# A graph kernel's last edge groups, its code copies and its last norms: four groups instead of three at the end, copies on POOL, norms on DVE and ACT

## The chip, the cores and the metric

The kernel runs on one core of a Trainium2 chip. Times are microseconds of device time of one execution. Several runs of each kernel are made, and their median is what is compared; one more execution is taken with the hardware profiler, and all rows, timelines and waits below are of that one.

The engines are PE (matrix products), DVE and ACT (elementwise work), POOL (GpSimd: elementwise work, and it issues the indirect DMAs) and SP, whose queue issues nearly all other DMAs.

## The reference

There are N = 6250 nodes with 128 features, and E = 206250 edges with 128 features each. Every edge adds its features to its source node; the sum enters a small dense network, a residual and a layer norm.

```python
edge_aggr = jnp.zeros((n, HIDDEN), dtype=x.dtype).at[row].add(edge_features)
combined = jnp.concatenate([x, edge_aggr, global_expand], axis=-1) @ W_c + b_c
h = jax.nn.softplus(combined @ W1 + b1)
h = jax.nn.softplus(h @ W2 + b2)
y = h @ W3 + b3
out = _layernorm(x + y, axis=-1)
```

All data is float32. The edges come in no order of their source node.

## The kernel before

**Edges as columns.** The edges are laid out as 1612 columns of 128 (one edge in each partition; the last column holds 42). The nodes are cut into 25 blocks of 256. The first 48 columns are summed directly: for each, ACT builds a one-hot matrix over all nodes (`direct_hot`, L577 and L579) and PE multiplies (L589). The other 1564 columns go through groups.

**Groups.** `GROUPS` (L23) lists (columns, `sub`). For each group, DVE works out from the node numbers where each edge has to stand so that the edges are sorted by block, each block padded to whole chunks of `sub` x 128 rows (`node_codes` L205, `positions` L243, a list of small steps). POOL then scatters the rows of each column with an indirect DMA to a region of HBM, `place` (`scatter_rows` L638, the scatter itself on L644). There are three such regions, used in turn (`place_of`), so a group's scatters wait until the group three before it has been read. A column is scattered as 129 numbers: 128 features and the edge's code, which says which node of its block it belongs to, counted from a number of the group's own (`code_of` L188). The code is copied into the loaded row tile by `code_rows` (L632, ACT).

**Reduction.** When all scatters of a group have landed, its chunks are read back (`load` L400, up to eight columns of chunks in one DMA, five buffers), each code is compared with 256 numbers (`match` L409: DVE on L423 in one instruction for all columns; in the last two groups three of four loads on ACT, one instruction a column on L418 and one for all on L420; three buffers `hot`), PE multiplies (L437, two matrix instructions a column in float32) and DVE adds each chunk's product to its block in `sums_t` (L454; the block's place is read into registers, L448). Two chunks share one of three PSUM buffers (`SUMS`). With `sub` = 4 a load holds two chunks, with 2 four, with 1 eight, so the smaller `sub` is, the less padding there is and the more additions.

**The order.** The columns of a group are handled in pieces of ten (`LOAD_COLS`); 159 pieces in all. The loop on L698 goes through groups and pieces: for each piece it loads rows three pieces ahead, copies codes two pieces ahead and scatters the piece; between pieces it spreads, each list by its share of the group's pieces (`AHEAD`): the next group's positions (`prep`), the reduction of the group before (`sums`), the direct work in groups 1 to 6, and other steps. PE, DVE, ACT and SP execute in the order written here; POOL's order is left to the framework. All DMAs of SP have one order. After the loop the last group is reduced (L738).

**Dense layers.** 13 tiles of 512 nodes (one of 106) go through two softplus layers and a last product (`z_of`, `decay`, `log1p`, `softplus`, `last_layer`), on PE, ACT and DVE. The tiles are in parts of 4, 3, 3, 2 and 1. When a part's last tile is through, `norm` (L814) works out the inverse deviations on DVE by a chain of twelve small instructions, then scales all blocks of the part: on POOL (L833), for the last part on DVE. Each tile then goes out by one or two DMAs.

Of the kernel before, what the change touches and what calls it, by code (L numbers as in the profile page):

```python
# [7 lines left out]
F32 = mybir.dt.float32  # L8
BF16 = mybir.dt.bfloat16
I32 = mybir.dt.int32  # L10
U8 = mybir.dt.uint8
AF = mybir.ActivationFunctionType
# [4 lines left out]
P = 128  # L17

BL = 2 * P
LOAD_COLS = 10  # L20
EPS = 1e-5

GROUPS = ((40, 1), (120, 2), (200, 4), (240, 4), (240, 4), (240, 4), (212, 4), (140, 2), (88, 2),  # L23
          (44, 1))
CHUNK_ROWS = 1024
# [22 lines left out]
def kernel(  # L48
# [36 lines left out]
    for size, sub in GROUPS:  # L85
        c1 = min(TC, c0 + size)
        if c1 > c0:
# [12 lines left out]

    iota_f = const.tile([P, WIDE], F32, name="iota_f")
    nc.gpsimd.iota(iota_f, pattern=[[1, WIDE]], base=0, channel_multiplier=0,
                   allow_small_or_imprecise_dtypes=True)
# [64 lines left out]
    with ExitStack() as phase:  # L168
# [74 lines left out]
        def positions(g):  # L243
# [5 lines left out]
            in_block, so_far, got = {}, {}, {}  # L249
            pos = per.tile([P, C_MAX], I32, name="pos")  # L250
            pos_of[g] = pos
# [102 lines left out]
            def chunk_map():  # L354

                small = ps.tile([P, 4, P], F32, name="small", bufs=2)
                end_t = per.tile([NB, 1], F32, name="end_t")
                nc.tensor.transpose(small[:NB, 0, :], got["end"], ident)
                nc.vector.tensor_copy(end_t, small[:NB, 0, :1])
                ended = per.tile([NB, NSC_MAX], F32, name="ended")  # L360
                nc.vector.tensor_scalar(ended[:, :nsc], chunk_i[:, :nsc], end_t, None,
                                        op0=ALU.is_ge)
                offs = per.tile([1, NSC_MAX], I32, name="offs", bufs=3)
                offs_of[g] = offs
                flat = ps.tile([P, 4, P], F32, name="small", bufs=2).rearrange("p a b -> p (a b)")
                nc.tensor.matmul(flat[:1, :nsc], ones[:NB, :1], ended[:, :nsc],
                                 start=True, stop=True)
                nc.vector.tensor_scalar(offs[:, :nsc], flat[:1, :nsc], float(NB - 1), float(BL),
                                        op0=ALU.min, op1=ALU.mult)
# [22 lines left out]
        def reduce_steps(g):  # L392
# [16 lines left out]
            def match(i):  # L409
# [3 lines left out]
                hot_of[i] = hot  # L413
                if g > G - 3 and i % 4 != 3:

                    codes = iota_f[:, int(code_of(g)):int(code_of(g)) + BL]
                    for j in range(m):
                        nc.scalar.activation(hot[:, j], codes, AF.Abs,  # L418
                                             bias=chunks[i][:, j, D:W], scale=-1.0)
                    nc.scalar.activation(hot[:, :m], hot[:, :m], AF.Relu, bias=ones[:, :1],  # L420
                                         scale=-1.0)
                    return
# [122 lines left out]
        def direct_steps():  # L545
# [26 lines left out]
            def compare(c, w, q):  # L572
                n = min(WIDE, NB * BL - w * WIDE)
                hot = direct_p.tile([P, QUAD, WIDE], F32, name="direct_hot", bufs=4)
                hot_of[c, w, q] = hot
# [56 lines left out]
        def code_rows(i):  # L632
            if i >= len(pieces):
                return
            g, c, k, r = pieces[i]
            nc.scalar.copy(rows_at[i][:r, :k, D:W], low[:r, c:c + k].unsqueeze(2))  # L636

# [14 lines left out]
        with tc.manual_schedule(engines={ET.PE, ET.DVE, ET.Activation, ET.SP}):  # L652
# [22 lines left out]
            node_codes(ND, c1)  # L675
            for i in range(LEAD - 1):
                code_rows(i)
            for step in positions(0):
# [11 lines left out]
            left = [0.0] * G  # L690
            for g in range(1, G - 3):
                left[g] = max(0.0, groups[g][1] - groups[g][0]
                              - groups[g - 1][3] * groups[g - 1][2] / 3 - (9 if 3 <= g < 6 else 0))
# [4 lines left out]
            for g in range(G):  # L698
                mine = [q for q in range(len(pieces)) if pieces[q][0] == g]
                prep = []  # L700
                if g + 1 < G:
                    prep = [lambda g=g: node_codes(*groups[g + 1][:2])] + positions(g + 1)
                sums = reduce_steps(g - 1) if g else []
# [8 lines left out]
                for q in mine:  # L712
                    load_rows(i + LEAD)
                    code_rows(i + LEAD - 1)
                    scatter_rows(i)
# [30 lines left out]
    order = tiles[-1:] + tiles[:-1]  # L746
    parts = [order[:4]] + [order[i:i + 3] for i in range(4, len(order) - 3, 3)]
    parts += [order[len(parts) * 3 + 1:-1], order[-1:]]
    h1, h2, sub_z, x_of = {}, {}, {}, {}
# [64 lines left out]
    def norm(now, last):  # L814
# [9 lines left out]
        for _ in range(3):  # L824
            nc.vector.tensor_mul(t, g, g)
            nc.vector.scalar_tensor_tensor(t, t, -0.5, v, op0=ALU.mult, op1=ALU.mult)
            nc.vector.scalar_tensor_tensor(g, t, 1.5, g, op0=ALU.add, op1=ALU.mult)  # L827

        engine = nc.vector if last else nc.gpsimd
        for n0, w, y, at in now["done"]:  # L830
            for lo, hi, r in blocks(w):
                for q in range(lo, hi):
                    engine.tensor_scalar(y[:r, q, :], y[:r, q, :], mv[:r, at + q, 0:1],  # L833
                                         rs[:r, 1, at + q:at + q + 1],
                                         op0=ALU.subtract, op1=ALU.mult)
                m0 = n0 + lo * P
# [60 lines left out]
```

## Time and profile before

| what | value |
|---|---|
| median of 3 runs | 2163.95 us (2160.82 to 2169.29) |
| the profiled execution's own time | 2166.67 us |
| its span | 2164.9 us |
| mean granted TensorE clock | 0.925 |
| PE, PE weight loads | 1789.7 us (83%), 1209.0 us (56%) |
| DVE | 1328.0 us (61%) |
| ACT | 912.7 us (42%) |
| POOL | 1560.2 us (72%) |
| scatters | 1564, the first at 25.57, the last at 2018.42 |
| first layer's first product | 2086.08 |

How to read the rows: a group of instructions is given as line, engine, operation, tile written and tiles read, then the number of instructions, a bar, their busy time in us and the mean duration of one in ns, a second bar, and the idle time of the engine just before them with what ended most of it. "issue" is time in which the engine waited for nothing that the profile shows. A row of a timeline is start, duration, engine, line, operation, tiles, shapes, the number of instructions that it merges, and in brackets the idle time before with what ended it. The row of digits gives the busy share in tenths in 40 equal slices of the span, some 54 us each. Matrix products are pipelined and their ends are modelled.

### The profile page before, as it was taken

Reading aid. Unit: us, or ns where it says so; the run is one execution under the profiler, and the core shown is the slowest. Engines: PE = TensorE matmul, PEld = TensorE weight load, DVE = VectorE, ACT = ScalarE, POOL = GpSimd, SP = SyncE. Lnnn points to the kernel's source line nnn. Section 1 sums busy time; section 2 is a strip of 40 time slices with the busy share of each in tenths; the row PEclk is TensorE's granted clock in tenths of the full one; section 3 lists DMA queues with packets and bytes.
Section 4 is the critical chain, followed back from the end, with each engine's and each line's share of the span. In section 5 each row is a group of like instructions: output and inputs, shape, how many; then the busy total and the mean of one; then the engine's idle time right before and its main releaser. Section 6 shows DMA issues by size and latency. Waiting matters only on the chain.

```text
span 2164.9 us, 22230 instructions
## 1 busy us (share of the span) xinstructions
PE 1789.7 (83%) x6415; PEld 1209.0 (56%) x6415; DVE 1328.0 (61%) x1923; ACT 912.7 (42%) x1350; POOL 1560.2 (72%) x1631
## 2 busy tenths in 40 slices
PE   3398788966889878999889998788998899688884
PEld 0144445534555555666556666556666778566752
DVE  7386457524656345675465855355755798796567
ACT  0476665653444335444353443353342000006964
POOL 5777777777777767777777777777777777777226
PEclk8699999987999999999999999999999999899997
DMA  9998788738786665676756666556766687776521
GB/s 299 303 313 270 216 256 251 231 101 262 213 225 189 194 193 148 188 207 188 198 173 180 194 190 175 169 167 189 202 198 170 211 245 227 214 213 199 151 75 60
DMA packets 415376, 435.50 MB, mean 201 GB/s; under 512 B 37743, under 2 KB 305766, under 8 KB 415254
## 3 DMA queue, kind: packets, MB, share of 16 engines
q1 hardware_dynamic: 365062, 330.71, 54.9%
q0 software_dynamic: 50048, 103.35, 14.4%
q8 instruction: 51, 0.84, 0.2%
q14 instruction: 71, 0.58, 0.1%
q10 hardware_dynamic: 144, 0.02, 0.0%
HBM read 260.90 MB, written 173.03 MB: 200 GB/s over the span
## 4 chain that ended last, share of the span: by engine, by line
PE 57%; DVE 15%; POOL 9%; issue 7%; DMA 6%; ACT 4%; DVEq 1%; SPq 0%; POOLq 0%; ACTq 0%
PE part L437 37%; PE direct_sum L589 16%; POOL place L644 8%; DVE hot L423 7%; DMA place<-rows,pos 4%; DVE sums_t L454 2%; ACT hot L418 2%; DVE so_far L316 1%; DVE sums_t L593 1%; DMA rows<-in_edge_attr 1%; DMA chunks<-place 1%; PE small L339 1%; POOL y L833 1%; DVEq L448 1%; DVE pos L350 1%
## 5 line engine op out<-in xcount | busy, mean ns | idle before, releaser
L644 POOL DMA_INDIRECT place<-rows,pos x1564 | 1503.2, 961 | 509.0 <-issue 443.5
L437 PE MATMUL part<-hot,chunks 128*128 128x256 f32 x4472 | 1106.0, 405 | 267.8 <-DVE hot L423 250.9
L437 PEld LDWEIGHTS part<-hot,chunks 128*128 128x128 f32 x4472 | 894.9, 203 | 507.8 <-DVE hot L423 310.5
L577 ACT ACTIVATE direct_hot<-iota_f,less 128x512 f32<-128x512 f32 (+1 forms) x624 | 404.6, 695 | 811.0 <-PE direct_sum L589 808.1
L423 DVE SCALAR_TENSOR_TENSOR hot<-chunks,iota_ps 128x2048 f32<-128x2048 f32 (+1 forms) x261 | 592.2, 2270 | 44.2 <-DMA chunks<-place 44.2
L589 PE MATMUL direct_sum<-direct_hot,direct_rows 128*128 128x512 f32 (+1 forms) x1248 | 559.0, 580 | 29.4 <-DMA direct_rows<-in_edge_attr 25.6
L454 DVE TENSOR_TENSOR sums_t<-sums_t,part 128x256 f32 x781 | 327.1, 419 | 133.3 <-PE part L437 110.8
L589 PEld LDWEIGHTS direct_sum<-direct_hot,direct_rows 128*128 128x128 f32 x1248 | 233.3, 190 | 232.2 <-issue 204.9
L579 ACT ACTIVATE direct_hot<-direct_hot,ones 128x1024 f32<-128x1024 f32 (+1 forms) x312 | 348.0, 1115 | 10.1
L593 DVE TENSOR_TENSOR sums_t<-sums_t,direct_sum 128x512 f32<-128x512 f32 (+1 forms) x52 | 34.7, 667 | 410.5 <-PE direct_sum L589 410.5
L636 ACT COPY rows<-src_i 128x10 f32<-128x10 f32 (+1 forms) x159 | 30.7, 196 | 360.3 <-DMA place<-rows,pos 328.9
L350 DVE TENSOR_REDUCE pos<-at 128x20 int32<-128x500 f32 (+2 forms) x80 | 87.0, 1087 | 2.7
L316 DVE TENSOR_TENSOR_SCAN so_far<-iota_ps,ib 128x1500 bf16<-128x1500 f32 (+5 forms) x29 | 85.7, 2955 | 0.0
L418 ACT ACTIVATE hot<-iota_f,chunks 128x256 f32<-128x256 f32 x156 | 64.2, 493 | 26.7 <-DMA chunks<-place 24.2
L845 POOL TENSOR_TENSOR x_sb<-x_sb,b_all 128x512 f32<-128x512 f32 (+1 forms) x13 | 15.2, 1219 | 67.8 <-DMA x_sb<-in_x 67.8
L348 DVE TENSOR_TENSOR at<-small,ib 128x500 f32<-128x500 f32 (+2 forms) x80 | 52.9, 661 | 4.2 <-PE small L339 3.5
L833 POOL TENSOR_SCALAR y<-y,mv,rs 128x128 f32<-128x128 f32 (+1 forms) x45 | 35.2, 796 | 19.9 <-DVE rs L827 19.0
L262 DVE TENSOR_TENSOR ib<-block,iota_ps 128x1500 bf16<-128x1500 bf16 (+5 forms) x29 | 44.2, 1550 | 0.0
L273 PE MATMUL small<-ib,ones_h 128*128 128x500 bf16 (+2 forms) x80 | 23.8, 406 | 23.9 <-DVE ib L262 23.9
L536 DVE TENSOR_SCALAR z_x<-small,z_bias 128x512 f32<-128x512 f32 (+1 forms) x13 | 9.3, 718 | 51.3 <-PE small L534 51.3
L335 PE MATMUL small<-so_far,ones_h 128*128 128x500 bf16 (+2 forms) x80 | 31.4, 393 | 11.1 <-DVE last L319 11.1
L420 ACT ACTIVATE hot<-hot,ones 128x2048 f32<-128x2048 f32 (+1 forms) x20 | 39.2, 1960 | 0.7
(115 smaller groups left out, 472.7 us busy)
## 6 DMA issues: line engine op xcount, KB each, us to landing
chunks<-place SPq DMA_DIRECT2D x278, 516.0 KB, 4.5
rows<-in_edge_attr SPq DMA_DIRECT2D x155, 640.0 KB, 6.7
place<-fill SPq DMA_DIRECT2D x252, 258.0 KB, 8.3
place<-rows,pos POOLq DMA_INDIRECT x1564, 4.5
x_sb<-in_x SPq DMA_DIRECT2D x24, 256.0 KB, 4.6
direct_rows<-in_edge_attr SPq DMA_DIRECT2D x4, 768.0 KB
out<-y SPq DMA_DIRECT2D x12, 256.0 KB, 2.2
chunks<-place SPq DMA_DIRECT2D x3, 258.0 KB, 3.2
```

What stands on the lines that cost most here:

```text
L316: nc.vector.tensor_tensor_scan(t, iota_ps[:, 1:2].to_broadcast([P, NB * n]), in_block[k][0], 0.0, op0=ALU.mult, op1=ALU.add)
L350: nc.vector.tensor_reduce(pos[:, a - c0 + j0:a - c0 + j1], at.rearrange("p b g -> p g b"), axis=mybir.AxisListType.X, op=ALU.add)
L418: nc.scalar.activation(hot[:, j], codes, AF.Abs, bias=chunks[i][:, j, D:W], scale=-1.0)
L423: nc.vector.scalar_tensor_tensor(hot[:, :m], chunks[i][:, :m, D:W].to_broadcast([P, m, BL]), code_of(g), iota_ps.unsqueeze(1).to_broadcast ...
L437: nc.tensor.matmul(part[:, s - q, :], t[:, s * sub + j, :D], hot[:, s * sub + j], start=(j == 0), stop=(j == sub - 1))
L454: nc.vector.tensor_add(here, here, part[:, s - q, :])
L577: nc.scalar.activation(hot[:, j, :n], iota_f[:, :n], AF.Abs, bias=less[:, w, c + q + j:c + q + j + 1], scale=-1.0)
L579: nc.scalar.activation(hot[:, :, :n], hot[:, :, :n], AF.Relu, bias=ones[:, :1], scale=-1.0)
L589: nc.tensor.matmul(sum_of[c, w][:, :n], rows_in[c][:, q + j, :], hot[:, j, :n], start=(q + j == 0), stop=(q + j == k - 1))
L593: nc.vector.tensor_add(here, here, sum_of.pop((c, w))[:, :n])
L644: s = nc.gpsimd.indirect_dma_start(out=dst, out_offset=bass.IndirectOffsetOnAxis(ap=at, axis=0), in_=rows[:r, j, :], in_offset=None)
L833: engine.tensor_scalar(y[:r, q, :], y[:r, q, :], mv[:r, at + q, 0:1], rs[:r, 1, at + q:at + q + 1], op0=ALU.subtract, op1=ALU.mult)
```

## The change

- The groups after the sixth are (226, 4), (130, 2), (72, 2), (38, 1), (18, 1) instead of (212, 4), (140, 2), (88, 2), (44, 1). There are eleven groups instead of ten.
- The positions of group 8 are worked out in the stage of group 6 already, and those of groups 9 and 10 two stages ahead (`SOONER`). A third position buffer and a fourth offset buffer hold them.
- ACT matches in the last three groups: every other load in the first of them, three of four in the last two (`TAIL`). The row of numbers that codes are compared with gets 768 entries instead of 512, and `direct_hot` three buffers instead of four to make room.
- Codes are copied by POOL instead of ACT, for each piece just before its scatters in the program.
- The dense part's parts are 4, 3, 3 and 3 tiles. In the last one the blocks are scaled by DVE and ACT in turn; ACT needs the negative mean times the inverse deviation (`minus`), one more small instruction.

```diff
-GROUPS = ((40, 1), (120, 2), (200, 4), (240, 4), (240, 4), (240, 4), (212, 4), (140, 2), (88, 2),
-          (44, 1))
+GROUPS = ((40, 1), (120, 2), (200, 4), (240, 4), (240, 4), (240, 4), (226, 4), (130, 2), (72, 2),
+          (38, 1), (18, 1))
+SOONER = 6
+TAIL = (2, 4, 4)
...
-    iota_f = const.tile([P, WIDE], F32, name="iota_f")
+    iota_f = const.tile([P, len(TAIL) * BL], F32, name="iota_f")
...
-            pos = per.tile([P, C_MAX], I32, name="pos")
+            pos = per.tile([P, C_MAX], I32, name="pos", bufs=3)
...
-                if g > G - 3 and i % 4 != 3:
+                share = TAIL[g - G] if g >= G - len(TAIL) else 1
+                if i % share != share - 1:
...
-                hot = direct_p.tile([P, QUAD, WIDE], F32, name="direct_hot", bufs=4)
+                hot = direct_p.tile([P, QUAD, WIDE], F32, name="direct_hot", bufs=3)
...
         def code_rows(i):
-            if i >= len(pieces):
-                return
             g, c, k, r = pieces[i]
-            nc.scalar.copy(rows_at[i][:r, :k, D:W], low[:r, c:c + k].unsqueeze(2))
+            nc.gpsimd.tensor_copy(rows_at[i][:r, :k, D:W], low[:r, c:c + k].unsqueeze(2))
...
-            for i in range(LEAD - 1):
-                code_rows(i)
...
-                if g + 1 < G:
-                    prep = [lambda g=g: node_codes(*groups[g + 1][:2])] + positions(g + 1)
+                for k in range(g + 1 + (g > SOONER), min(G, g + 2 + (g >= SOONER))):
+                    prep += [lambda k=k: node_codes(*groups[k][:2])] + positions(k)
...
                     load_rows(i + LEAD)
-                    code_rows(i + LEAD - 1)
+                    code_rows(i)
                     scatter_rows(i)
...
-    parts = [order[:4]] + [order[i:i + 3] for i in range(4, len(order) - 3, 3)]
-    parts += [order[len(parts) * 3 + 1:-1], order[-1:]]
+    parts = [order[:4]] + [order[i:i + 3] for i in range(4, len(order), 3)]
...
-        engine = nc.vector if last else nc.gpsimd
+        if last:
+            minus = work.tile([P, 16], F32, name="minus")[:, :nb]
+            nc.vector.scalar_tensor_tensor(minus, mv[:, :nb, 0], -1.0, g,
+                                           op0=ALU.mult, op1=ALU.mult)
...
-                    engine.tensor_scalar(y[:r, q, :], y[:r, q, :], mv[:r, at + q, 0:1],
-                                         rs[:r, 1, at + q:at + q + 1],
-                                         op0=ALU.subtract, op1=ALU.mult)
+                    k = at + q
+                    if last and q % 2:
+                        nc.scalar.activation(y[:r, q, :], y[:r, q, :], AF.Identity,
+                                             bias=minus[:r, k:k + 1], scale=g[:r, k:k + 1])
+                        continue
+                    (nc.vector if last else nc.gpsimd).tensor_scalar(
+                        y[:r, q, :], y[:r, q, :], mv[:r, k, 0:1], g[:r, k:k + 1],
+                        op0=ALU.subtract, op1=ALU.mult)
```

The range over which direct work is spread keeps the groups 1 to 6 (`G - 4` for `G - 3`).

More of the change, by code (lines that the diff above doesn't have):

```diff
@@ L98 @@
     dram = ctx.enter_context(tc.tile_pool(name="dram", bufs=1, space=bass.MemoryType.DRAM))
-    iota_f = const.tile([P, WIDE], F32, name="iota_f")
-    nc.gpsimd.iota(iota_f, pattern=[[1, WIDE]], base=0, channel_multiplier=0,
+    iota_f = const.tile([P, len(TAIL) * BL], F32, name="iota_f")
+    nc.gpsimd.iota(iota_f, pattern=[[1, len(TAIL) * BL]], base=0, channel_multiplier=0,
                    allow_small_or_imprecise_dtypes=True)
@@ L362, in chunk_map @@
                                         op0=ALU.is_ge)
-                offs = per.tile([1, NSC_MAX], I32, name="offs", bufs=3)
+                offs = per.tile([1, NSC_MAX], I32, name="offs", bufs=4)
                 offs_of[g] = offs
@@ L690 @@
             left = [0.0] * G
-            for g in range(1, G - 3):
+            for g in range(1, G - 4):
                 left[g] = max(0.0, groups[g][1] - groups[g][0]
```

## The prediction

> **What bounds the kernel now.** I read the page first, for the share of each engine and its row in forty slices.
>
> ```profile
> span 2164.9 us, 22230 instructions
> ...
> POOL 5777777777777767777777777777777777777226
> ...
> L644 POOL DMA_INDIRECT place<-rows,pos x1564 | 1503.2, 961 | 509.0 <-issue 443.5
> ...
> L454 DVE TENSOR_TENSOR sums_t<-sums_t,part 128x256 f32 x781 | 327.1, 419 | 133.3 <-PE part L437 110.8
> ...
> L636 ACT COPY rows<-src_i 128x10 f32<-128x10 f32 (+1 forms) x159 | 30.7, 196 | 360.3 <-DMA place<-rows,pos 328.9
> ```
>
> PE is busiest (83%), but POOL's row does not move: seven tenths in every slice until the 37th, then almost nothing. The timeline of POOL tells why.
>
> ```profile
> 25.57 1.20 POOL L644 DMA_INDIRECT place<-rows,pos  x1 [18.45 <-DMA w_sb<-in_L_gnn_W]
> 27.08 0.96 POOL L644 DMA_INDIRECT place<-rows,pos  x1 [0.31 <-issue]
> ...
> 801.28 0.96 POOL L644 DMA_INDIRECT place<-rows,pos  x1 [0.30 <-issue]
> 811.52 0.96 POOL L644 DMA_INDIRECT place<-rows,pos  x1 [9.28 <-ACT rows L636]
> 812.78 0.96 POOL L644 DMA_INDIRECT place<-rows,pos  x1 [0.30 <-issue]
> ...
> 2017.16 0.96 POOL L644 DMA_INDIRECT place<-rows,pos  x1 [0.31 <-issue]
> 2018.42 0.91 POOL L644 DMA_INDIRECT place<-rows,pos  x1 [0.30 <-issue]
> 2086.94 0.45 POOL L845 TENSOR_TENSOR x_sb<-x_sb,b_all 106x128 f32<-106x128 f32 x1 [67.61 <-DMA x_sb<-in_x]
> ```
>
> One scatter starts every 1.265 us (2017.16 to 2018.42), busy 0.96 and 0.30 in which it waits for nothing shown. 1564 of them run from 25.6 to 2019.3. The sum of real waits in that stretch is about 15 us: 9.28 here, 1.46 at 1432.7 (both for the code copy on ACT), 4.63 at 81.2 (a load of rows). So POOL alone sets when the last edge is placed, although the chain of waits gives it 9%; PE, DVE and ACT have slack until then. The span is 25.6 of start, 1993.8 of scatters, 66.6 until the last sum is added (2085.9), and 79.0 of the dense layers.
>
> For the 66.6 us I read the timelines of ACT and DVE.
>
> ```profile
> 1969.43 3.30 ACT L418 ACTIVATE hot<-iota_f,chunks 128x256 f32<-128x256 f32 x8 [24.15 <-DMA chunks<-place]
> 1972.76 2.00 ACT L420 ACTIVATE hot<-hot,ones 128x2048 f32<-128x2048 f32 x1
> ```
>
> ```profile
> 1957.08 2.28 DVE L423 SCALAR_TENSOR_TENSOR hot<-chunks,iota_ps 128x2048 f32<-128x2048 f32 x1
> 1959.27 1.85 DVE L454 TENSOR_TENSOR sums_t<-sums_t,part 128x256 f32 x4
> 1961.04 2.28 DVE L423 SCALAR_TENSOR_TENSOR hot<-chunks,iota_ps 128x2048 f32<-128x2048 f32 x1
> ...
> 2065.20 3.88 DVE L454 TENSOR_TENSOR sums_t<-sums_t,part 128x256 f32 x8 [0.45 <-PE part L437]
> 2069.53 3.81 DVE L454 TENSOR_TENSOR sums_t<-sums_t,part 128x256 f32 x8 [0.45 <-PE part L437]
> 2073.80 1.85 DVE L454 TENSOR_TENSOR sums_t<-sums_t,part 128x256 f32 x4 [0.45 <-PE part L437]
> ...
> 2084.08 1.86 DVE L454 TENSOR_TENSOR sums_t<-sums_t,part 128x256 f32 x4 [0.20 <-DVE sums_t L454]
> ```
>
> Per load of eight columns: a match on ACT takes 5.23 us, on DVE 2.19 start to start; PE needs 3.57 (64 multiplications in 14.27). In groups of two columns a chunk DVE turns a load round in 3.96 when it matches too; in single chunks its eight adds take 4.3 and the match comes on top. ACT runs without a gap from 1969.4 to 2069.1 and then DVE's adds are last.
>
> **The code copies.** This decides the sign. They leave ACT (159, 0.196 us each, and 329 us in which ACT stood before them) and join the one queue that has no slack. What ACT gains is worth only what POOL waited for it: 9.28 + 1.46 less two usual gaps of 0.30 = **10.1 us** off. The 4.63 us for rows stays. What the copies add on POOL, no row shows. The nearest by size is the IOTA of 128x13 (142 ns, writes only); from the tensor additions (454 ns at 128 elements, 1.22 us start to start at 512: 2.0 ns an element) ten elements would come to 0.22. The scatter behind a copy has to wait for it, and a scatter that ACT released at 811.25 (its copy's end) began at 811.52: 0.27 after. That replaces the 0.30 it would have had anyway. So a copy that starts as the scatter ends costs 0.14 + 0.27 - 0.30 = 0.11; with 0.22 busy, 0.19. The bounds: 0, if it runs inside the 0.30 of the scatter before (below nothing is excluded: no work leaves POOL); and 0.30 + 0.22 + 0.27 - 0.30 = 0.49, if it too starts only after such a gap. Compute instructions that follow one another on POOL leave none (the normalisations start every 0.785 us at 0.796 busy), so I take the row nearest in size: 0.11 x 159 = **17.5 us**, between 0 and 78.
>
> The Trainium skill speaks against the lower bound. "Perfetto Trace Analysis", section "GPSIMD Engine Instruction", says that spans of this engine are not to be trusted and that start-to-start spacing is. By the rows there are 0.30 us idle per scatter to hide a copy in, and the edit is free; by the rule the 1.265 is all work and each copy is paid. I go with the rule, hence 0.11 rather than 0. "SBUF — State Buffer", section "Who interferes with whom", adds that a GpSimd instruction that reads SBUF is blocked by a DVE one with two SBUF inputs. Copies read, scatters' times hardly vary. Here such DVE work is rare (L199, L202, L298: 0.2 to 0.3 us, three a group); matches and adds read one operand from PSUM. By the rule at worst thirty collisions of 0.3 us, 9 us; by that share of DVE's time under 1. I add nothing.
>
> A copy waits for its load of rows, with all later scatters queued behind it, but those waited for the same load before. At the start the copies' inputs are there by 9.2, scatters begin at 25.6: nothing.
>
> **The groups.** Padding makes 2262 columns of products, 26 more: 12 us of PE over the run, hidden in stages that POOL paces. Only the end counts (numbers from zero; the 0.11 is in POOL's times).
> - Group 7 (130) has 89 chunks, 23 loads. Before, 24 loads and the positions of 44 columns took DVE 111.1 us (1858.6 to 1969.7), from 6.3 after the last scatter. Now one load and three quarters of another go, 7 us, and the positions of 18 columns cost some 3 less: 101. POOL needs 72 x 1.265 + 0.9 = 92 for group 8. So group 7's sums end 15 after that group's last scatter (6 before the change).
> - Group 8 (72): 60 chunks, 15 loads, half matched on ACT (5.23 per two) and half on DVE: PE's 3.57 bounds, 54 us. It ends 69 later; POOL's groups 9 and 10 take 48.5 + 23.1 = 71.6. So 3 us before the last scatter.
> - Groups 9 and 10 (38, 18): 62 + 42 single chunks. DVE: 12 full loads of 4.27, rests of 3.3 and 1.4, three matches of 2.19: 62.6. ACT: 11 matches, under 57, earlier begun; PE: 104 x 0.446 = 46. DVE is last.
> The sums end 60 us after the last scatter instead of 66.6: **6.5 off**. Fewer single columns are left over than the shift suggests: 104 single chunks take the place of 68.
>
> Group 6 grows by two loads and its positions' stage takes in group 8's; its backlog of some 20 us of PE at the start of the next stage (direct sums until 1691) could push all this by 5; bounds of the 6.5 are 0 and 15.
>
> **Buffers.** A position buffer more and one `direct_hot` less: nothing. A compare takes ACT 2.45 us, and 314 steps in some 1590 us leave 5 between two; ACT stands 808 us before that buffer as it is. Without that cover PE would fall behind and scatters would wait for the place of three groups ago. The wider iota is 0.27 us at 0.8, first read at 9.1: nothing. Earlier positions move DVE work inside POOL's time.
>
> **Norms.** The chain before the last tile (2148.3 to 2150.9) goes, so its addition starts 2.6 earlier; then 12 reciprocal roots (2.4 as at 2138.4), one more small operation (0.2), twelve blocks, six each on DVE (0.33 a start) and ACT (about 0.3, from 0.28 for 106 columns): 2.0. Normalisation ends at about 2154.8, not 2157.5 (POOL's last); one output issue instead of two is left behind it (0.92 for two). **3 off**; 0 to 4, since three tiles now leave at once.
>
> **The sum.** +17.5 - 10.1 - 6.5 - 3 = -2.1. The profiled execution took 2166.67, 1.8 outside its span; it would be 2164.6. The median of the runs is 2.7 lower: 2163.95 - 2.1 = **2162**.
>
> **The rivals.** *The copy breaks the queue (slower).* Each copy starts only after a scatter's full gap, or reads slower than the small rows: 0.30 us each is 47.7, so +28 and 2192; at the bound of 0.49 it is 2222. It decides from 0.124 us a copy (19.6 / 159), and from 0.19 it is visible. For it: scatters leave 0.30 after themselves without exception. Against: sequencer waits run while a scatter runs, and small POOL instructions follow closely. *Copies vanish in the gap (faster).* At zero, -19.6 and 2144. If DVE's adds also keep up with PE (46 for 62.6), the tail loses 16 more: 2128. For it: 0.30 idle as shown; against: the rule above, and 4.3 a load measured. *The split doesn't help:* if the backlog of groups 6 to 8 eats the 6.5, 2168; no sign change.
>
> **Chances.** A measurement tells 0.5% (10.8 us) from no change. Likeliest, copies of 0.05 to 0.18: 2152 to 2174, chance 0.37. Queue broken, above that: 0.32. Copies nearly free, or a shorter tail: 0.31. The range takes in most of both others, 2142 to 2193.
>
> **What would show it.** The spacing between the last scatter of a piece and the first of the next, less 1.265, times 159, is the copies' price. Waits for ACT rows must be gone and the last scatter end near 2027. After it the sums should take 60, with DVE's adds last; the stretch from there to the end 76. I am wrong if a copy costs over 0.19 or the sums take under 50.

## The result, and the profile after

Over 12 runs each the changed kernel took 2157.81 us (2154.09 to 2160.67) and the kernel before 2163.51 (2158.13 to 2169.29): a ratio of 0.9973, interval 0.9962 to 0.9984, or 5.7 us less. The forecast was 2162, with 2.1 us off. The profiled execution took 2160.67 with a span of 2158.9, at a granted clock of 0.941 (0.925 before).

| stretch, profiled, us | before | forecast | after |
|---|---|---|---|
| end of the last scatter | 2019.3 | 2026.7 | 2020.0 |
| from there to the last sum | 66.6 | 60 | 68.1 |
| from the last sum to the end of the span | 79.0 | 76 | 70.7 |

So the total was near, and all three rows are off in these two profiles, by 6.7, 8.1 and 5.3 us, the middle one against the other two: the last scatter came earlier than forecast, the stretch after it did not shrink, and the end took less. How far the granted clock bears on such times is not settled: of 26 executions of the kernel before on one chip the six at a clock under 0.935 took no longer than the others (medians of 2169.0 and 2168.5 us), of 21 on another the eight under it took 4 us longer (2172.1 and 2167.9).

The views that answer to those of before: first POOL's waits (wait, total us, times, longest), one row of the kernel before and then the changed kernel.

```profile
POOL place L644 <- ACT rows L636: 12.3, 7, 9.3
```

```profile
POOL place L647 <- issue: 412.5, 1353, 0.3
...
POOL place L647 <- POOL rows L639: 19.0, 122, 0.2
...
POOL place L647 <- DMA rows<-in_edge_attr: 5.6, 1, 5.6
```

No row for ACT is left; in its place stand 122 short waits of a scatter for POOL's own copy. POOL's timeline shows one:

```profile
1996.26 0.96 POOL L647 DMA_INDIRECT place<-rows,pos  x1 [0.30 <-issue]
1997.23 0.20 POOL L639 COPY rows<-src_i 128x7 f32<-128x7 f32 x1
1997.59 0.98 POOL L647 DMA_INDIRECT place<-rows,pos  x1 [0.16 <-POOL rows L639]
1998.87 0.96 POOL L647 DMA_INDIRECT place<-rows,pos  x1 [0.30 <-issue]
...
2019.14 0.90 POOL L647 DMA_INDIRECT place<-rows,pos  x1 [0.31 <-issue]
```

The copy starts when the scatter ends, takes 0.20 to 0.21, and the next scatter follows 0.16 later. That 0.37 stands where 0.30 of gap would have been: the spacing is 1.33 (1996.26 to 1997.59) and not 1.263. Over 112 single copies the median price is 0.063 us; the framework placed 16 pairs (0.183 each) and a few larger bunches. All copies together cost some 11 us.

Then DVE at the end of the sums: group 6's last addition and group 7's first match, first in the kernel before, then in the changed kernel, where the last additions follow.

```profile
1850.31 0.42 DVE L454 TENSOR_TENSOR sums_t<-sums_t,part 128x256 f32 x1 [0.85 <-PE part L437]
...
1858.64 2.29 DVE L423 SCALAR_TENSOR_TENSOR hot<-chunks,iota_ps 128x2048 f32<-128x2048 f32 x1 [4.00 <-DMA chunks<-place]
```

```profile
1865.64 0.42 DVE L459 TENSOR_TENSOR sums_t<-sums_t,part 128x256 f32 x1 [0.85 <-PE part L442]
...
1868.34 4.48 DVE L428 SCALAR_TENSOR_TENSOR hot<-chunks,iota_ps 128x2048 f32<-128x2048 f32 x2
...
1971.00 2.28 DVE L428 SCALAR_TENSOR_TENSOR hot<-chunks,iota_ps 128x2048 f32<-128x2048 f32 x1
...
2083.11 3.81 DVE L459 TENSOR_TENSOR sums_t<-sums_t,part 128x256 f32 x8 [0.46 <-DVE sums_t L459]
2087.31 0.88 DVE L459 TENSOR_TENSOR sums_t<-sums_t,part 128x256 f32 x2 [0.39 <-DVE sums_t L459]
```

In the changed kernel group 6's last addition is at 1865.6, group 7 begins at 1868.3 and fills DVE for 102.7 us until 1971.0, and the last addition ends at 2088.2. In between PE works through group 8 without a pause (240 products), and group 9's first load follows:

```profile
1971.04 52.07 PE L442 MATMUL part<-hot,chunks 128*128 128x256 f32 x240 [0.61 <-ACT hot L425]
2023.40 3.72 PE L442 MATMUL part<-hot,chunks 128*128 128x256 f32 x16 [0.29 <-ACT hot L425]
```

These are nearly the lengths that the prediction gave (101, 54 and 62.6 us; measured 102.7, 52.1 and 63.6, from 2024.6 on). Above all the start of the chain was later than assumed. Group 7's last scatter ended at 1852.4 before and at 1857.2 after the change. Before, group 6's sums were through by then (1850.7) and group 7 began 6.2 us later; after, they ended 8.8 us past it and group 7 began 11.1 us later.

### The profile page after: what moved, and what is told of

Its sections match the earlier page's. It is cut to its first block, busy times and chain, and to the rows that moved or that the text cites. A ratio compares the mean times of both kernels' runs of the same rounds, so it can differ in the third digit from the quotient of the medians.

```text
span 2158.9 us, 21792 instructions
## 1 busy us (share of the span) xinstructions
PE 1804.2 (84%) x6470; PEld 1217.8 (56%) x6470; DVE 1351.9 (63%) x1976; ACT 889.6 (41%) x1186; POOL 1583.0 (73%) x1782
## 4 chain that ended last, share of the span: by engine, by line
PE 57%; DVE 15%; POOL 9%; DMA 8%; issue 6%; ACT 3%; SPq 1%; DVEq 1%; ACTq 0%; POOLq 0%
PE part L442 39%; PE direct_sum L594 14%; POOL place L647 8%; DVE hot L428 7%; DMA place<-rows,pos 4%; DVE sums_t L459 3%; DMA place<-fill 3%; DVE sums_t L598 1%; SPq L149 1%; DMA rows<-in_edge_attr 1%; ACT hot L423 1%; DVE so_far L320 1%; PE small L343 1%; DVEq L453 1%; ACT away L776 0%
## 5 line engine op out<-in xcount | busy, mean ns | idle before, releaser
L442 PE MATMUL part<-hot,chunks 128*128 128x256 f32 x4524 | 1117.4, 405 | 245.7 <-DVE hot L428 237.3
L442 PEld LDWEIGHTS part<-hot,chunks 128*128 128x128 f32 x4524 | 905.4, 203 | 484.7 <-DVE hot L428 294.3
L428 DVE SCALAR_TENSOR_TENSOR hot<-chunks,iota_ps 128x2048 f32<-128x2048 f32 (+1 forms) x266 | 602.6, 2266 | 45.5 <-DMA chunks<-place 45.5
L594 PE MATMUL direct_sum<-direct_hot,direct_rows 128*128 128x512 f32 (+1 forms) x1248 | 562.9, 582 | 35.2 <-DMA direct_rows<-in_edge_attr 26.3
L459 DVE TENSOR_TENSOR sums_t<-sums_t,part 128x256 f32 x808 | 338.0, 418 | 99.9 <-PE part L442 74.2
L594 PEld LDWEIGHTS direct_sum<-direct_hot,direct_rows 128*128 128x128 f32 x1248 | 232.2, 190 | 243.8 <-issue 199.0
L584 ACT ACTIVATE direct_hot<-direct_hot,ones 128x1024 f32<-128x1024 f32 (+1 forms) x312 | 348.0, 1115 | 10.1
L354 DVE TENSOR_REDUCE pos<-at 128x20 int32<-128x500 f32 (+3 forms) x80 | 87.0, 1088 | 2.7
L320 DVE TENSOR_TENSOR_SCAN so_far<-iota_ps,ib 128x1500 bf16<-128x1500 f32 (+7 forms) x30 | 85.9, 2863 | 0.0
L352 DVE TENSOR_TENSOR at<-small,ib 128x500 f32<-128x500 f32 (+3 forms) x80 | 52.8, 660 | 11.6 <-PE small L343 10.7
L266 DVE TENSOR_TENSOR ib<-block,iota_ps 128x1500 bf16<-128x1500 bf16 (+7 forms) x30 | 44.3, 1502 | 0.0
L277 PE MATMUL small<-ib,ones_h 128*128 128x500 bf16 (+3 forms) x80 | 23.7, 405 | 24.5 <-DVE ib L266 24.5
L339 PE MATMUL small<-so_far,ones_h 128*128 128x500 bf16 (+3 forms) x80 | 31.5, 394 | 11.2 <-DVE last L323 11.2
```

Of the source, the lines that this page charges most:

```text
L320: nc.vector.tensor_tensor_scan(t, iota_ps[:, 1:2].to_broadcast([P, NB * n]), in_block[k][0], 0.0, op0=ALU.mult, op1=ALU.add)
L352: nc.vector.tensor_mul(at, got.pop((k, j0)), in_block[k][1][:, :, j0:j1])
L354: nc.vector.tensor_reduce(pos[:, a - c0 + j0:a - c0 + j1], at.rearrange("p b g -> p g b"), axis=mybir.AxisListType.X, op=ALU.add)
L428: nc.vector.scalar_tensor_tensor(hot[:, :m], chunks[i][:, :m, D:W].to_broadcast([P, m, BL]), code_of(g), iota_ps.unsqueeze(1).to_broadcast ...
L442: nc.tensor.matmul(part[:, s - q, :], t[:, s * sub + j, :D], hot[:, s * sub + j], start=(j == 0), stop=(j == sub - 1))
L459: nc.vector.tensor_add(here, here, part[:, s - q, :])
```

## The experiments

Twelve kernels ran, on four chips. On two of them the kernel before took 2168.7 and 2168.0 us. On the other two it took 2842 and 2864 us, at granted clocks of 0.82 to 0.84; four of the five runs made there stand at the end. Ratios are always to the kernel before on the same chip.

### Norms alone

The kernel before with the new last part (three tiles, blocks scaled by DVE and ACT in turn) and nothing else of the change.

> The kernel before with the new last part alone (three tiles, blocks on DVE and ACT). Theory A (the whole gain of the change is here, since POOL no longer does the last blocks, and the copies on POOL cancel the waits they remove): 2155 to 2158, ratio to the kernel before 0.997, and 71 to 73 us from the last sum to the end where before took 79.0. Theory B (the forecast: the norms are worth 3): 2160.5.

Measured: 2163.38 us, ratio 0.9978 (0.9969 to 0.9987), that is 4.8 us off (2.8 to 6.7); from the last sum to the end 69.5 us. The times of both theories assumed a kernel before of 2163, and it took 2168.7 on this chip. Taken as gains, theory A's 6 to 7 us and theory B's 3 both lie in the interval. The stretch speaks for theory A: 69.5, where the forecast's was 76. Whether all of the change's 5.7 us lies here the interval can't say.

### The old groups

The changed kernel, with the ten groups:

```diff
...
-          (226, 4), (130, 2), (72, 2), (38, 1), (18, 1))
+          (212, 4), (140, 2), (88, 2), (44, 1))
-SOONER = 6
-TAIL = (2, 4, 4)
+SOONER = 99
+TAIL = (4, 4)
...
-            for g in range(1, G - 4):
+            for g in range(1, G - 3):
```

The three `direct_hot` buffers and the added position and offset buffers stay.

> The changed kernel with the ten groups of before (and their positions one stage ahead, ACT matching three of four loads in the last two). Theory A (the new groups gave nothing: the last sums come 68 us after the last scatter with them, 67 with the old ones): within 3 us of the changed kernel, 2155 to 2161. Theory B (the forecast's step: the groups alone are worth 6.5): 2164 or more, and sums 73 us after the last scatter. Both hold where the kernel before takes about 2163; where it does not, the stretch from the last scatter to the last sum is what is read.

Measured: 2166.54 us, ratio 0.9993 (0.9984 to 1.0002). The stretch from the last scatter to the last sum is 66.9 us: theory A's number, and the expectation names this stretch as what is read where the kernel before does not take about 2163 (it took 2168.7). By the ratios, the kernel is 0.0020 slower than the changed one (0.9973, measured elsewhere), 4.3 us with 3.1 either way: between theory A (at most 3) and theory B (6.5), and neither is ruled out. So the profile shows no gain of the new groups, and the medians point to a small one.

### Codes copied by ACT

The changed kernel with the codes copied as before, two pieces ahead:

```diff
...
-            nc.gpsimd.tensor_copy(rows_at[i][:r, :k, D:W], low[:r, c:c + k].unsqueeze(2))
+            nc.scalar.copy(rows_at[i][:r, :k, D:W], low[:r, c:c + k].unsqueeze(2))
...
-                    code_rows(i)
+                    code_rows(i + LEAD - 1)
```

> The changed kernel with the codes copied by ACT, two pieces ahead, as before; all else stays. Theory A (copies on POOL cost 12 us and take away 11 to 23 of waits for ACT): last scatter within 5 us of the changed kernel's 2020, POOL's waits for ACT rows 10 to 25 us, total within 5 of it. Theory B (the copies are pure cost): last scatter 10 us earlier, total 2147. Theory C (POOL copies are the whole gain): 8 us slower or more.

Measured: 2160.41 us where the kernel before took 2167.95, ratio 0.9959 (0.9943 to 0.9975). The waits for ACT are back. The first row is of this kernel, the second of norms alone, which has its copies on ACT too:

```profile
POOL place L649 <- ACT rows L641: 14.8, 8, 7.4
```

```profile
POOL place L644 <- ACT rows L636: 23.3, 7, 10.2
```

With the kernel before's 12.3 us these waits lie between 12 and 23 us in the three profiles, about what the copies on POOL cost: theory A.

**Four kernels together.** All have the new norms. The one with old groups and codes by ACT is norms alone, with four `direct_hot` buffers; the other three have three.

| ratio to the kernel before | codes by ACT | codes by POOL |
|---|---|---|
| old groups | 0.9978 | 0.9993 |
| new groups | 0.9959 | 0.9973 |

Each column gives the groups: -0.0019 and -0.0020, the mean -0.0020 with some 0.0012 either way (from the four intervals), 4.2 us. Each row gives the copies: +0.0015 and +0.0014, 3.1 us with 2.5 either way. That both columns agree, and both rows, shows that the two edits hardly act on each other, and that the fourth buffer shows no effect. (That norms, groups and copies add up to the whole change, -4.8, -4.2 and +3.1 us, follows from the table by arithmetic and confirms nothing.)

Two things weaken the small differences. Only the first row is known to compare kernels on one chip; the other comparisons take ratios from one set of runs to another, and that these carry over at this size is not shown. And among executions at a granted clock above 0.935 alone, the ratio with new groups and codes by ACT is 0.9965 and that of norms alone 0.9974, so that this column would give the groups half as much.

### Copies twice

Every code copied twice, one copy straight after the other:

```diff
+            for _ in range(2):
-            nc.gpsimd.tensor_copy(rows_at[i][:r, :k, D:W], low[:r, c:c + k].unsqueeze(2))
+                nc.gpsimd.tensor_copy(rows_at[i][:r, :k, D:W], low[:r, c:c + k].unsqueeze(2))
```

> The changed kernel with every code copied twice by POOL, one copy after the other; nothing is left out. Theory A (what is paid is POOL's time: a second copy next to a first adds 0.12 us, as in the changed kernel's pairs): last scatter at 2039, total 19 us longer, some 2177. Theory B (a copy's price is the hand-over to the next scatter, paid once a piece): last scatter within 5 us of 2020. Theory C (the forecast's slower rival, 0.30 us for each): 48 us longer.

Measured: 2246.66 us, ratio 1.0364 (1.0348 to 1.038); the last scatter ends at 2112.4, 92 us later than in the changed kernel, more than any of the three theories gave. POOL's timeline of this kernel:

```profile
479.80 0.95 POOL L648 DMA_INDIRECT place<-rows,pos  x1 [0.30 <-issue]
480.75 0.47 POOL L640 COPY rows<-src_i 128x10 f32<-128x10 f32 x2
481.76 0.98 POOL L648 DMA_INDIRECT place<-rows,pos  x1 [0.53 <-issue]
```

A pair costs 1.96 - 1.263 = 0.70 us (0.68 median of 112 pairs), not 0.18. The second copy writes what the first wrote, and by the semaphores in the trace it waits on the first in all 159 pairs; the scatter behind it carries no wait on POOL in 119 of 124 cases, and starts 0.53 us after the copies rather than 0.16. The edit had changed the waits, not only doubled a cost.

### Half copies

Each copy in two halves that do not touch, so that the second waits for nothing and the scatter waits as in the changed kernel:

```diff
-            nc.gpsimd.tensor_copy(rows_at[i][:r, :k, D:W], low[:r, c:c + k].unsqueeze(2))
+            for a, b in ((0, k // 2), (k // 2, k)):
+                if a < b:
+                    nc.gpsimd.tensor_copy(rows_at[i][:r, a:b, D:W],
+                                          low[:r, c + a:c + b].unsqueeze(2))
```

> The changed kernel with each code copy made in two halves, five columns each, that do not touch each other; nothing is left out. Theory A (a further copy that waits for nothing costs 0.12 us, as in the changed kernel's pairs; the 0.6 us of the second copy in the run with copies twice came from its wait for the first one): last scatter 19 us later than in the changed kernel, 2037 to 2042. Theory B (every further copy costs 0.5 to 0.6): 80 us later. Theory C (the price goes by elements): within 5 us of the changed kernel.

Measured: 2177.04 us, ratio 1.0034 (1.002 to 1.0048); the last scatter ends at 2040.9, 20.8 later: theory A. The timeline, where two pieces' halves were bunched:

```profile
482.39 0.96 POOL L650 DMA_INDIRECT place<-rows,pos  x1 [0.31 <-DMA place<-rows,pos]
483.35 0.56 POOL L641 COPY rows<-src_i 128x5 f32<-128x5 f32 x4
484.06 0.98 POOL L650 DMA_INDIRECT place<-rows,pos  x1 [0.15 <-POOL rows L641]
```

Four copies take 0.56 together, 0.12 to 0.13 for each further one, and the scatter again follows 0.15 later. A pair costs 0.174 (median of 111). Of the 0.51 by which the pairs with a wait cost more, 0.14 lies in the copies (0.47 together where these take 0.33) and 0.37 between them and the scatter; why the scatter is late there, without a wait on POOL, is not shown.

The two kernels also price a later scatter. Against the changed kernel, 20.8 us later cost 0.0061 (some 0.0018 either way), 13 us; the next 71.6 us later cost 0.0330 (some 0.0021 either way), 71 us. The stretch after the last scatter shrinks from 68.1 to 63.1 and 56.4 us. The first step can be read in this run's profile: with the scatters later, group 6's sums were through (1876.2) when group 7's last scatter ended (1876.6), and group 7 began 6.7 us after it, not 11.1. So 4 to 5 us of the stretch of 68.1 were group 6's sums, which DVE still owed. In the second step the medians give nearly the full delay, though the stretch shrinks by another 6.7 in the profiles.

### Direct sums earlier

```diff
+            left[6] *= 0.7
             direct_at = 0.0
```

> The changed kernel with three tenths of the direct sums of group 6's stage spread over those of groups 1 to 5; nothing is left out. Some 42 us of matrix products leave that stage, in which PE ran on to 1709 where the scatters of group 6 were done. Theory A (the end of the sums was late by what PE had left over from that stage): group 7's first match comes 10 to 15 us earlier than 1868, and the last sum 8 to 15 us earlier than 2088; total 2143 to 2150. Theory B (the sums of the last two groups are bound by their own 104 additions after the last scatter): last sum within 3 us of 2088, total unchanged. Against both: PE falls behind in an earlier stage and the scatters wait for the place of three groups ago, slower by 5 or more.

Measured: 2165.64 us, ratio 0.9982 (0.9973 to 0.9991), no better than the changed kernel. None of theory A's gain came. PE's timeline where the direct sums (L594) end, first in the changed kernel, then in this one:

```profile
1705.89 3.91 PE L594 MATMUL direct_sum<-direct_hot,direct_rows 128*128 128x256 f32 x16
1714.77 23.13 PE L442 MATMUL part<-hot,chunks 128*128 128x256 f32 x96 [4.97 <-DVE hot L428]
```

```profile
1712.32 2.75 PE L594 MATMUL direct_sum<-direct_hot,direct_rows 128*128 128x256 f32 x12
1720.21 20.09 PE L442 MATMUL part<-hot,chunks 128*128 128x256 f32 x82 [5.14 <-DVE hot L428]
```

They end no earlier against the scatters: 17.9 us after group 6's last scatter in the changed kernel (1691.9), 18.1 here (1697.0), though this stage has 152 of these products where the changed kernel has 196. (The last scatter was 5.5 us later too, half of it at the start of the run.) Group 7 begins at 1873.6, 11.1 after that group's last scatter in both kernels, and the last sum comes 67.9 after the last scatter. PE was not full in this stage: it stood idle for 31 us of 287 in the changed kernel and for 40 here. So the edit did not take the left-over away, theory A stays untested by it, and what keeps the sums of this stage until 18 us after its scatters is not shown.

### ACT matches in group 7

```diff
-TAIL = (2, 4, 4)
+TAIL = (2, 2, 4, 4)
```

> The changed kernel with ACT matching every other load of group 7 too (TAIL 2, 2, 4, 4); nothing else. In the changed kernel ACT does nothing from 1750 to 1970 while DVE matches and adds group 7 in 102.7 us. Theory A (the end of the sums is a chain, group 7 on DVE, then group 8 on PE, then the additions of groups 9 and 10, and it is late by what group 7 takes): group 7 takes some 83 us (23 loads of 3.57), its end moves from 1971 to about 1951, and the last sum comes 15 to 20 us earlier, some 50 after the last scatter in place of 68; total 2138 to 2144, ratio to the kernel before 0.988 to 0.991. Theory B (the last additions alone are bound, or ACT's slower matches hold PE up): last sum within 4 us of 68 after the last scatter, total unchanged.

Measured: 2162.12 us, ratio 0.9959 (0.9943 to 0.9974), against 0.9973 (0.9962 to 0.9984) for the changed kernel: not told apart. The stretch is 63.6 us and not 68.1, with the last scatter 5.3 us later and the last sum 0.7 later than in the changed kernel; the kernel with the direct sums earlier, whose scatters ended as late, had 67.9. So the direction is theory A's and the size is not. ACT and PE of this kernel show where the gain went:

```profile
1874.54 3.30 ACT L423 ACTIVATE hot<-iota_f,chunks 128x256 f32<-128x256 f32 x8 [158.06 <-DVE wrap L215]
```

```profile
1879.93 13.40 PE L442 MATMUL part<-hot,chunks 128*128 128x256 f32 x48 [7.36 <-ACT hot L425]
...
1969.61 53.75 PE L442 MATMUL part<-hot,chunks 128*128 128x256 f32 x240 [2.38 <-ACT hot L425]
```

Group 7 takes 90 us on PE (1879.9 to 1969.6), where the changed kernel takes 100 (1870.7 to 1971.0). But group 6's last addition came 7 us later in this run (1872.6; group 7's scatters ended 5.2 later), PE stood 7.4 us for ACT's first match, and group 8 and the last additions took their 54 and 65 us as before.

### A late operation on POOL

The changed kernel with a copy of one column on POOL behind the last norm's small chain:

```diff
+            late = work.tile([P, 1], F32, name="late")
+            nc.gpsimd.tensor_copy(late, minus[:, :1])
```

> The changed kernel with one copy of one column on POOL behind the last small DVE instruction of the norms, 2.6 us after POOL's last work in the changed kernel; its result is not used. Theory A (POOL's drain ends 6.6 us after its last compute instruction and the program's end waits for it): POOL's drain ends about 2160, the span is longer by about 2 us, and all other engines stand before the end. Theory B (the drain only looks long because POOL had nothing else to do): the end follows the output DMAs as it did, span unchanged to 0.3.

One execution of 2970.33 us, on a chip on which the kernel before takes 2842; only its end is read here. The end of its timeline:

```profile
2960.58 1.62 DVE L843 TENSOR_SCALAR y<-y,mv,rs 128x128 f32<-128x128 f32 x6
2960.72 0.24 POOL L834 COPY late<-minus 128x1 f32<-128x1 f32 x1 [2.14 <-DVE minus L831]
2960.74 2.42 ACT L840 ACTIVATE y<-y,minus,rs 128x128 f32<-128x128 f32 x6 [7.20 <-DVE minus L831]
```

The span ends at 2968.40: 7.44 us after POOL's copy, and 5.2 after ACT's last block. In the changed kernel ACT's last block is 3.2 before the end:

```profile
2141.43 9.31 POOL L841 TENSOR_SCALAR y<-y,mv,rs 128x128 f32<-128x128 f32 x12 [4.77 <-DVE rs L827]
...
2153.14 1.62 DVE L841 TENSOR_SCALAR y<-y,mv,rs 128x128 f32<-128x128 f32 x6
2153.31 2.42 ACT L838 ACTIVATE y<-y,minus,rs 128x128 f32<-128x128 f32 x6 [7.11 <-DVE minus L831]
```

(ACT ends at 2155.73, the span at 2158.89.) Three runs with the new norms on the chip of this run end 3.2 to 3.4 us after ACT's last block, so the 5.2 is not the chip's. In the kernel before POOL's last block ended at 2157.46 and the span 7.43 later.

What lies between is POOL's closing drain, an instruction at the end of the program that does not count as busy. Its rows in the kernel before, the changed kernel and this one, in that order (number, then shortest, median and longest in ns, then the first and the last start):

```profile
L893 POOLq DRAIN  x3: 40/107/12675, 2151.4 to 2164.6; - x3
```

```profile
L901 POOLq DRAIN  x3: 40/107/15548, 2141.8 to 2158.6; - x3
```

```profile
L903 POOLq DRAIN  x3: 40/107/6893, 2960.7 to 2968.1; - x3
```

The longest is the first. It ends at 2164.1, 2157.4 and 2967.6: each time 6.6 us after POOL's last compute instruction. SP, which issues the output's DMAs, was through with its waits at 2160.8, 2158.1 and 2965.5. So the drain was last by 3.3 us in the kernel before. With the blocks on DVE and ACT, POOL is done at 2150.7 and its drain is through 0.7 before SP. With 0.24 us of late work on POOL it is last again, by 2 us: theory A.

### Where the kernel before takes 2842 to 2864 us

The times of four kernels stand here. Why all kernels take this long on these two chips was not looked into, and none of it explains the result above.

> The kernel before with the new norms alone (parts of 4, 3, 3, 3 tiles, the last one scaled by DVE and ACT). Theory A, from the two traces: the whole gain sits here, since POOL's closing drain ends 6.6 us after POOL's last compute instruction and that instruction comes 6.5 us earlier; the span after the last sum goes from 79.0 to about 72, the time down by 6 to 7, to 2157. Theory B, the prediction's sums: the norms give 3 us, the time is about 2160.5, and the rest of the 5.7 comes from elsewhere.

Norms alone: ratio 0.9963 (0.9926 to 1.0), and 71.4 us from the last sum to the end.

> The changed kernel with the ten old groups, their order of positions and ACT's share of before (new copies and norms stay). Theory A: the new groups are worth nothing, as the sums end 68 us after the last scatter in place of 66.6; the time is 2156 to 2158, within 2 us of the changed kernel, and its sums end 66 to 67 after the last scatter. Theory B, the prediction: the new groups take 6.5 us off, so without them the time is about 2164.

Old groups, codes by POOL: 2951.35 us, ratio 1.0399 (1.0352 to 1.0445).

> The changed kernel with the code copies back on ACT, two pieces ahead, as before (new groups and norms stay). Theory A: 159 copies cost POOL about 12 us in the changed trace and ACT's lateness cost it 10 before, so the last scatter ends within 3 us of 2020; but ACT's copies now stand before its matches in three groups, so the sums end later than 68 us after the last scatter; time 2158 to 2165. Theory B, the prediction: copies cost 17.5 and save 10, so the last scatter ends 7 earlier and the time is about 2151.

New groups, codes by ACT: 2795.92 us, ratio 0.9831 (0.9778 to 0.9884). These two kernels' first rows of POOL's waits, in that order:

```profile
POOL place L647 <- DMA rows<-in_edge_attr: 653.0, 57, 31.4
```

```profile
POOL place L649 <- ACT rows L641: 516.1, 72, 17.3
```

Here POOL waits for hundreds of microseconds, for rows in the one and for ACT in the other, and neither number of the expectations can be read from it. Of the change itself this much can be read. The changed kernel with one late copy on POOL took 2970.33 us on this chip, in one execution, 4.5% more than the kernel before; with its codes copied by ACT it took 1.7% less. So the gain above is shown only where the kernel before takes some 2165 us; on this chip the change, as far as that one execution tells, is a loss.

> The changed kernel with the codes copied by ACT two pieces ahead, as before, and ACT matching every other load of group 7 too: both edits that came out at 0.9959 of the kernel before. Theory A (they add up: the copies on POOL cost 3 us, group 7 on DVE alone another 3): ratio 0.993 to 0.995. Theory B (they collide: in the stage in which ACT now matches group 7, the copies stand behind matches of 5.2 us that wait for chunks, and POOL with its scatters behind the copies): waits of POOL for ACT rows above 25 us, the last scatter 5 or more later, ratio 0.996 or above.

Codes by ACT and ACT matching in group 7: 2837.25 us where the kernel before took 2864.09, ratio 0.9883 (0.9828 to 0.9938), with 613.7 us of waits for ACT rows. Whether the two edits add up where the kernel before takes some 2165 us stays open, and with it whether a version beats the changed kernel beyond doubt.

## Why the prediction was right, and where its steps were not

- **Copies: the sign right, the term mis-sized.** Forecast 0.11 us each, 17.5 in all; measured 0.063 for a single one, 0.07 on average, 11 in all. Two parts of the 0.11 were off, in opposite directions: the copy is busy 0.21 (I took 0.14; the 0.22 from the tensor additions was right), and the scatter follows 0.156 after it, not the 0.27 seen behind a copy on ACT. The rule of the Trainium skill that I leaned on ("Perfetto Trace Analysis", section "GPSIMD Engine Instruction": spacing, not spans) gave the right way to measure, but my reading of it, that the 1.265 is all work, is too strict: a copy and its hand-over take 0.37, and 0.30 of that lies where a gap stood. The step's net was +7.4; the four kernels give +3.1, with 2.5 either way.
- **Waits for ACT:** gone, as forecast. They were 12 us in the profile of before and 15 to 23 in others with copies on ACT, so 10.1 was at the low end.
- **Collisions with DVE:** I added nothing for them, and none shows. The 159 copies on POOL took 0.19 to 0.26 us.
- **The queue breaking:** 0.30 for each copy did not happen. The run with copies twice shows that such a price exists, 0.68 a pair, where the second copy waits for the first and the scatter starts late.
- **Groups: not by the step that I gave.** "The sums end 60 us after the last scatter instead of 66.6" failed: 68.1 after, and 66.6 to 67.6 in the three profiles with the old groups. The lengths of the pieces were nearly right, the beginning was not. I let group 7's sums end 15 us after group 8's last scatter (1948.9); they ended 22 after it. Of these 7 us, 4.8 are a late start: group 6's sums ran past their stage and held DVE until 1866. I had named 5 us for just this backlog and put it at nothing in the sum. Another 1.7 are a longer group 7. Behind it, 1.5 between group 8's last product and the next addition had been left out. That group 6 had grown by 14 columns, and the stage in which its sums run had shrunk by ten, fits the backlog but is not shown to be its whole cause: with the old groups and codes by POOL these sums ran 4.0 us past group 7's last scatter, with the new groups and codes by ACT 1.7. In the latter the stretch was 67.3 all the same, as group 7 took 2 us longer. Nor is the stretch a constant that POOL leaves behind: it shrinks when the scatters come later. The medians give the new groups 4.2 us, with 2.5 either way and the reservations above. Where such a gain would lie the single profiles, whose own times stand up to 8 us from their medians, do not show; this stays open.
- **Norms: the direction right, a term left out.** Forecast 3, measured 4.8 by the medians with norms alone (2.8 to 6.7, so that 3 is just inside), and 69.5 to 72.4 us for the end in eight profiles with the new norms, where I had 76. I counted the chain and the blocks, and took DVE, ACT and the output as last. POOL's drain, 6.6 us after its last block, was last before, by 3.3 us; I had seen no row for it. Of the 8.3 us that the first two profiles show in this stretch, some 1.7 are the first layer's first products, which were slower in the profile of before (1.85 and 1.91 us, where they took 1.02 to 1.04 after).
- **The bound.** "POOL alone sets when the last edge is placed" is right for the scatters. "PE, DVE and ACT have slack until then" is not: group 6's sums ran past their stage. So POOL's time reaches the end only in part: 13 of the first 20.8 us by the medians, and nearly all of what comes after. The forecast took every microsecond in full, for the copies and for the waits alike.
- **Luck in the total.** In the profiles the last scatter came 6.7 us earlier than forecast and the end was 5.3 shorter, while the sums took 8.1 longer. The forecast's copies were too dear and its norms too small, both of which made it too long, and its groups gave too much, which made it too short. That the total came within 4 us owes something to this.

## What to carry to other kernels

Before a stretch after the last event of a queue is taken as a constant, ask what other engines still owe at that moment: delay the queue on purpose once, and see what of the delay reaches the end. A small operation put between queued ones is priced by start-to-start spacing and by what it waits for, not by its busy time. At the end of a program look at which engine was used last and how long it takes to close, not only at which did the last useful work.

## What the runs showed of the hardware

- A POOL copy of 128x10 that feeds the next scatter costs 0.063 us between two indirect DMAs; each further copy that waits for nothing 0.11 to 0.13; with a second copy that waits for the first, and a scatter that starts 0.53 after it, a pair costs 0.68.
- A scatter follows POOL's own copy after 0.156 us, and a copy on ACT after 0.27.
- POOL's closing drain ended 6.6 us after POOL's last compute instruction, in four profiles alike. The span ended 7.4 us after that instruction where it came late, and 3.2 to 3.4 us after ACT's last block where POOL was done before.
- The plain spacing of scatters was 1.266 us in the profile of before, 1.263 in that of after, and 1.263 to 1.265 in seven more profiles on chips where the kernel before takes some 2168 us, with copies on either engine. Over 1563 scatters 0.003 is 4.7 us; it does not go with the engine of the copies, and its cause was not found.
